# Which queue carries the loads, and where cproj's tiles live, in a fused cross-attention block

## The chip, the core and the metric

The kernel runs on one core of a Trainium2 chip. The metric is the device time of one execution in microseconds, the median of several runs. The engines are TensorE (PE; its weight loads are listed as PEld), VectorE (DVE), ScalarE (ACT), GpSimd (POOL) and SyncE (SP, which only issues DMAs; its queue is listed as SPq).

## The reference

A transformer block with cross-attention, in float32, for 4 batches. Queries and context have 512 rows of 512 features, there are 16 heads of 32, and the inner size of the MLP is 2048:

```python
x = layer_norm(hidden_states, ln1_w, ln1_b)
q = split_heads(x @ q_w + q_b)
k = split_heads(encoder_hidden_states @ k_w + k_b)
v = split_heads(encoder_hidden_states @ v_w + v_b)
attn = softmax(where(mask, q @ k.T / sqrt(32), min))
hidden = merge_heads(attn @ v) @ cproj_w + cproj_b + hidden_states
y = layer_norm(hidden, ln2_w, ln2_b)
return hidden + gelu(y @ fc_w + fc_b) @ proj_w + proj_b
```

## The kernel before, in words

**Groups, tiles, pairs.** The attention work is cut into 16 groups of four heads: group `w` is batch `w // 4`, heads `4 * (w % 4)` on. Each group has four query tiles of 128 rows. For each tile `scores` (L228) multiplies q and k on TensorE (`sc`, L235), VectorE adds the mask and takes the minimum (L240; q is negated, so this is the row's maximum), and ScalarE takes the exponential and its sum (L244). The probabilities must then be transposed for the product with v. In two of the pairs (`ON_PE`) TensorE does that (`turn`, L258) and ScalarE and VectorE copy the result into a `tb` buffer (L261, L263). Everywhere else VectorE transposes blocks of 32 by 32 into `tb` (L272, and L280 for the sums), and then sixteen DMAs per pair of tiles, each of 136 KB, exchange the block rows between partitions (`exchange`, `copies`, L314), from `tb` into `pT`, `gt` or `xe`. A pair is two query tiles, so there are 32 pairs, numbered 0 to 31: pair 7 is the second half of group 3. There are two `tb` buffers, so a new one is free only when the exchange out of an older one has landed. `attend` (L337) multiplies v with the transposed probabilities (`av`, L357), in most cases four tiles after the pair's first tile.

**What runs in between.** Other work is put between the score tiles: the k, q and v products (`prep_k`, `prep_q`, `prep_v`: L196, L205, L217) of later groups, layer norm 1 of the next batch (`ln1`, its transposes `tp` at L137), the cproj products of a finished batch (`cproj`, L390 on), layer norm 2, and the MLP of batches 0 and 1 (`fc` L454, `proj` L464). The order is written out by hand in the lists `first[w]` and `later[w]` (L762 to L833) and run by the loop from L836: each entry has a cost, 3.4 for a chain of matmuls and 0.5 for a set of transposes, and before and after each `turn` the loop runs as many entries as half a tile's share of the group's cost allows. Loads have cost 0. The last two batches' MLPs come after the attention, in a form with fewer products (`last_mlps`).

**Queues.** The exchanges are issued by SyncE. A load is issued by whatever engine `Q[0]` names when the program is written: GpSimd for groups 0 to 3, SyncE from group 4 on (L836 to L839). The first batch's loads are on SyncE. Each engine issues its DMAs in program order, together with its other instructions. On GpSimd these are additions of a bias row (`add_row`, L369, 128 by 512), the bias of v (L224) and the reciprocal root of the layer norms (`ln_rs`). `prep_q` and `prep_v` load the next group's wq and wv right after their own matmuls (L206, L221) since there is one buffer of each; wk has two buffers and is loaded at the head of `A(w)`.

**x, rows and cproj.** Layer norm 1's x tiles are allocated from the pool `tiles`, tag `xn`, four buffers (`load_x`, L152). In group 3 the list ends with `hid_(0, ...)`, which loads the four residual tiles of batch 0 and adds a bias row to each (L371), and then `load_x` of batch 2 (`x1`, L800). cproj of batch 0 works on these residual tiles. For batches 1 and 2 it works on `ct` tiles from a pool with two buffers: two are loaded ahead, and the third and fourth are loaded by GpSimd after the store of the first and second (L400 to L402). Their bias rows are added inside `cproj` (L392 to L394). All four results are stored to a DRAM tensor `xa`, from where `load_yn` (L404) and `load_hid` read them again. cproj's weights `wc` (1 MB) are loaded by GpSimd ahead of group 0 (L835). The MLP's weights pass through a ring of eight 256 KB buffers (`load_mlp`, L439); the first eight, all of fc, are loaded at the end of group 0's list.

Of the kernel before, what the change touches and what calls it, by code (L numbers as in the profile page):

```python
# [36 lines left out]
F32 = mybir.dt.float32  # L37
# [7 lines left out]
P = 128  # L45
B, L, D, H = 4, 512, 512, 16
HD = D // H
INNER = 4 * D
NT = L // P
# [25 lines left out]
def xattn_block(ctx: ExitStack, tc: tile.TileContext, x, encT, mask, q_w, k_w, v_w, c_w, fc_w, p_w, vecs, rows, out):  # L75
    nc = tc.nc
    scale = float(np.float32(1.0) / np.sqrt(HD).astype(np.float32))

    def pools(stack, **bufs):
        return [stack.enter_context(tc.tile_pool(name=n, bufs=k)) for n, k in bufs.items()]  # L80

    const, keep, hids, tiles, small = pools(ctx, const=1, keep=1, hids=6, tiles=4, small=4)
    dram = ctx.enter_context(tc.tile_pool(name="dram", bufs=1, space=bass.MemoryType.DRAM))
# [3 lines left out]
    one, two, kqp, five, six, fws = pools(att, one=1, two=2, kqp=4, five=5, six=6, fws=MW)  # L87
# [9 lines left out]
    wc = one.tile([P, ND, D], F32, tag="wc", name="wc")  # L97
# [7 lines left out]
    S = {}  # L105
    Q = [nc.gpsimd]

    def acc_tile(name):
        return ps_acc.tile([P, D], F32, tag="acc", name=name)
# [61 lines left out]
    def load_mask(b, queue):  # L171
        queue.dma_start(out=m8, in_=mask[b : b + 1, :].broadcast_to([P, L]))

    def make_mb(b):
        mb = one.tile([P, L], F32, tag="mb", name=f"mb_{b}")
        nc.vector.tensor_scalar(mb, m8, 0.0, FMAX, ALU.is_equal, ALU.mult)
        if b + 1 < B:
            load_mask(b + 1, nc.gpsimd)
        S["mb", b] = mb

    def load_w(w, queue=None, names=("wk", "wq", "wv")):

        if w >= NW:
            return
        g = w % NG
        for n, src in (("wk", k_w), ("wq", q_w), ("wv", v_w)):
            if n in names:
                S[n, w] = (two if n == "wk" else one).tile([P, ND, P], F32, tag=n, name=f"{n}_{w}")
                (queue or Q[0]).dma_start(out=S[n, w], in_=src[:, g, :, :])

    def prep_k(w):
        b, g = divmod(w, NG)
        kT = kqp.tile([P, L], F32, tag="kT", name=f"kT_{w}")
        acc = acc_tile(f"acck_{w}")
        for d in range(ND):
            nc.tensor.matmul(acc, S["wk", w][:, d, :], eT[:, d, :], start=(d == 0), stop=(d == ND - 1))  # L196
        nc.scalar.activation(kT, acc, AF.Identity, bias=vec[:, KB + g : KB + g + 1], scale=1.0)
        S["kT", w] = kT

    def prep_q(w):  # L200
        b, g = divmod(w, NG)
        qT = kqp.tile([P, L], F32, tag="qT", name=f"qT_{w}")
        acc = acc_tile(f"accq_{w}")
        for d in range(ND):
            nc.tensor.matmul(acc, S["wq", w][:, d, :], xT[:, d, :], start=(d == 0), stop=(d == ND - 1))  # L205
        load_w(w + 1, names=("wq",))  # L206

        nc.scalar.activation(qT, acc, AF.Identity, bias=qb[:, g : g + 1], scale=-scale)
        S["qT", w] = qT

    def prep_v(w):
        b = w // NG
        v = five.tile([P, NT, P], F32, tag="v", name=f"v_{w}")
        acc = acc_tile(f"accv_{w}")
        for t in range(NT):
            for d in range(ND):
                nc.tensor.matmul(  # L217
                    acc[:, ts(t, P)], eT[:, d, ts(t, P)], S["wv", w][:, d, :],
                    start=(d == 0), stop=(d == ND - 1),
                )  # L220
        load_w(w + 1, names=("wv",))  # L221
        nc.scalar.copy(v, acc.rearrange("p (t f) -> p t f", t=NT))  # L222
        bias = row[:, 2, ts(w % NG, P)]
        nc.gpsimd.tensor_tensor(v, v, bias[:, None, :].broadcast_to([P, NT, P]), ALU.add)  # L224
        S["v", w] = v
# [142 lines left out]
    def add_row(h, i):  # L368
        nc.gpsimd.tensor_tensor(h, h, row[:, i, :], ALU.add)  # L369
# [7 lines left out]
        for t in ts_:  # L377
            add_row(S["hid", b, t], 1 if b else 0)

    def load_ct(b, t, queue=None):  # L380

        if t == 0:
            S["xa", b] = dram.tile([L, D], F32, tag=f"xa{b}", name=f"xa{b}")
        if b == B - 1:
            S["ct", b, t] = tiles.tile([P, D], F32, tag="xn", name=f"ct_{b}_{t}")
        else:
            S["ct", b, t] = two.tile([P, D], F32, tag="ct", name=f"ct_{b}_{t}")
        (queue or Q[0]).dma_start(out=S["ct", b, t], in_=x[b, ts(t, P), :])

    def cproj(b, t):  # L390
        h = S["hid", b, t] if b == 0 else S["ct", b, t]
        if b:  # L392
            for i in range(NT if b == B - 1 else 2) if t == 0 else (t,) if t > 1 and b < B - 1 else ():
                add_row(S["ct", b, i], 0)  # L394
        acc = acc_tile(f"accc_{b}_{t}")
        for g in range(NG):
            nc.tensor.matmul(acc, S["oT", b][:, g, ts(t, P)], wc[:, g, :], start=(g == 0), stop=(g == NG - 1))  # L397
        nc.vector.tensor_tensor(h, acc, h, ALU.add)
        if b:
            (nc.sync if b == B - 1 else nc.gpsimd).dma_start(out=S["xa", b][ts(t, P), :], in_=h)  # L400
            if t + 2 < NT and b < B - 1:
                load_ct(b, t + 2, nc.gpsimd)  # L402

    def load_yn(b):  # L404

        S["yn", b] = [tiles.tile([P, D], F32, tag="xn", name=f"xn2_{b}_{t}") for t in range(NT)]
        for t in range(NT):
            Q[0].dma_start(out=S["yn", b][t], in_=S["xa", b][ts(t, P), :])

    def stat2(b, t):  # L410
# [281 lines left out]
    CHAIN, TURN = 3.4, 0.5  # L692

    def do(fn):
        return [(0.0, fn)]

    def A(w):
        if w >= NW:
            return []
        return do(lambda: load_w(w + 1, names=("wk",))) + [  # L700
            (CHAIN, lambda: prep_k(w)),
            (CHAIN, lambda: prep_q(w)),
            (CHAIN, lambda: prep_v(w)),
        ]

    def C(b):
        return [(CHAIN, lambda t=t: cproj(b, t)) for t in range(NT)]
# [54 lines left out]
    first = [[] for _ in range(NW)]  # L762
    later = [[] for _ in range(NW)]
    x1, x2, x3, x4 = inputs(1)
    load2, k2, q2, v2 = A(2)
    load3, k3, q3, v3 = A(3)
    load4, k4, q4, v4 = A(4)
    first[0] = do(lambda: load_w(2, names=("wk",))) + [(CHAIN, lambda: prep_v(1)), (CHAIN, lambda: prep_q(1))] + x1 + [load2, k2, q2] + do(load_mlp)
    first[1] = x2[:1] + [v2, load3, k3] + x2[1:2] + [q3] + x2[2:] + [v3] + x4 + x3
    first[2] = [load4, q4, k4, v4] + A(5)[:2]  # L770
    first[3] = A(5)[2:] + A(6)
    mlp = []
    for p in range(NORMAL):
# [2 lines left out]
    def some(n):  # L776
        taken, mlp[:n] = mlp[:n], []
        return taken

    def hid_(b, *ts_):  # L780
        return do(lambda: load_hid(b, ts_))

    def ct(b):
        return do(lambda: (load_ct(b, 0), load_ct(b, 1)))

    def yn(b):
        return do(lambda: load_yn(b))
# [9 lines left out]


    x1, x2, x3, x4 = inputs(2)
    first[3] += hid_(0, 0, 1, 2, 3) + x1  # L800
    load, k, q, v = A(7)
    c, t2 = C(0), turns2(0)
    first[4] = [load, k] + x2[:2] + [q] + x2[2:] + [v] + x3[:2] + x4
    later[4] = c[:1] + x3[2:] + c[1:]
    load, k, q, v = A(8)
    first[5] = stat(0, 0, 1) + [load, q] + stat(0, 2, 3) + rs(0) + [k] + norm(0, 0, 1, 2, 3) + [v]
    first[5] += t2 + do(lambda: proj_bias(0)) + some(5)
    load, k, q, v = A(9)
    x1, x2, x3, x4 = inputs(3)
    first[6] = [load, k, q] + some(5) + [v] + x1  # L810
    load, k, q, v = A(10)
    first[7] = [load, k, q] + some(5) + [v]

    load, k, q, v = A(11)
    first[8] = ct(1) + [load, k] + x2[:1] + [q] + x2[1:2] + some(1) + x2[2:] + [v] + x3[:2] + x4
    c = C(1)
    later[8] = c[:1] + x3[2:] + c[1:]
    load, k, q, v = A(12)
    first[9] = [load, q] + some(2) + [k] + some(3) + [v]
    load, k, q, v = A(13)  # L820
    first[10] = [load, k, q] + some(5) + [v] + yn(1)
    load, k, q, v = A(14)
# [2 lines left out]
    first[11] += norm(1, 2, 3) + some(1) + t2 + [v] + some(1)  # L825

    load, k, q, v = A(15)
    c = C(2)
    first[12] = ct(2) + [load, k] + some(3) + hid_(1, 0, 1)
    later[12] = c  # L830
    first[13] = hid_(1, 2, 3) + [q] + some(3) + [v] + some(3)
    first[14] = yn(2) + some(5) + stat(2, 0, 1) + some(2) + stat(2, 2, 3) + rs(2) + some(1)
    first[15] = norm(2, 0, 1) + some(4) + norm(2, 2, 3) + some(4) + turns2(2)  # L833

    nc.gpsimd.dma_start(out=wc, in_=c_w)  # L835
    for w in range(NW):  # L836
        if w and w % NG == 0:
            make_mb(w // NG)
            Q[0] = nc.sync  # L839
        work, rest = first[w], later[w]  # L840
        share = sum(c for c, _ in work + rest) / NT
        due = 0.0
        for qt in range(NT):
            u = w * NT + qt
            pair = AT.get(u, (u - LAG) // 2 if u >= LAG and u % 2 == 0 else None)
            if pair in AT.values() and u not in AT:
                pair = None
            if pair is not None:
                turn_sums(*divmod(pair, 2))
                attend(*divmod(pair, 2))  # L850
            scores(w, qt)

            if qt == 2:
                work, rest = work + rest, []
            due += share / 2
            due -= run(work, due)
            turn(w, qt)
            if u % 2 == 1:
                over_sums(w, qt // 2)
            due += share / 2  # L860
            due -= run(work, due)
        run(work + rest)
    exchange()

    for t in range(NT):
        load_ct(B - 1, t)
    run(some(2))
    turn_sums(NW - 1, 0)
    attend(NW - 1, 0)
# [56 lines left out]
```

## Time and profile before

| | us |
|---|---|
| median of 3 runs (836.4 to 838.74) | 836.82 |
| the profiled execution | 840.83 |
| its span, first to last instruction | 839.0 |
| TensorE busy | 811.6 (97%) |
| VectorE busy | 553.9 (66%) |
| ScalarE busy | 342.5 (41%) |
| GpSimd busy | 119.6 (14%) |
| mean granted TensorE clock | 0.987 |

All places are microseconds from the start of the profiled span. The page cuts the span in 40 slices of 21 us, and gives the busy share of each in tenths. In a timeline each row has the start, the length, the engine, the line, the operation with output and inputs, how many instructions were merged, and in brackets the idle time of the engine just before and what ended it. DMA rows on SPq or POOL are the issuing, not the transfer.

### The profile page before, as it was taken

The page shows a single profiled execution, that of the slowest core. Times are in us where ns is not written, and L with a number is a line of the kernel's source. Part 1 is how long each engine was busy: PE and PEld are TensorE (multiplying, and loading weights), DVE is VectorE, ACT ScalarE, POOL GpSimd, SP SyncE. Part 2 cuts the span into 40 slices and gives each one's busy share as a digit, 9 for nine tenths or more (in the row PEclk, how much of TensorE's full clock was granted, in tenths as well). Part 3 has the DMA queues.
Part 4 walks back from the last instruction along what each step waited for, and adds up shares of the span by engine and source line. Part 5 has one row for each costly group of instructions (what it writes and reads, how often), then busy time and mean ns, then how long its engine had stood idle before and what let it go on. Part 6 is the DMA issues. An engine that isn't in the chain of part 4 may idle for free.

```text
span 839.0 us, 11999 instructions
## 1 busy us (share of the span) xinstructions
PE 811.6 (97%) x4064; PEld 472.3 (56%) x4064; DVE 553.9 (66%) x1259; ACT 342.5 (41%) x740; POOL 119.6 (14%) x152
## 2 busy tenths in 40 slices
PE   9997999499999999999999989999999999999998
PEld 6545544345445454454554435443446888888887
DVE  4595887577666786776787476787425998168511
ACT  2654554134764564356444456464301331023300
POOL 2332214303000013100001321000022003100011
PEclk9997999799999999999999999999999999999999
DMA  5477488565777877587786867985835551032001
GB/s 205 164 194 184 136 243 217 147 165 145 186 189 198 227 198 226 157 211 187 197 240 166 249 167 185 237 194 136 226 119 194 168 181 46 8 94 75 14 14 38
DMA packets 57885, 136.88 MB, mean 163 GB/s; under 512 B 12144, under 2 KB 14320, under 8 KB 57696
## 3 DMA queue, kind: packets, MB, share of 16 engines
q1 hardware_dynamic: 52176, 117.75, 51.9%
q0 software_dynamic: 5120, 17.24, 6.8%
q10 hardware_dynamic: 528, 1.14, 0.6%
q8 instruction: 32, 0.52, 0.3%
q14 instruction: 29, 0.24, 0.1%
HBM read 61.89 MB, written 7.34 MB: 83 GB/s over the span
## 4 chain that ended last, share of the span: by engine, by line
PE 83%; DMA 7%; DVE 5%; SPq 2%; POOL 2%; issue 1%; ACT 0%; DVEq 0%; POOLq 0%
PE accp L464 13%; PE accf L454 12%; PE q L558 12%; PE sc L235 7%; PE av L357 7%; PE accv L217 5%; PE accc L397 5%; PE accq L205 5%; PE acck L196 4%; DMA pT<-tb 2%; PE tp L137 2%; DMA xn<-x_dram 2%; PE q4p L598 2%; PE q6p L598 2%; PE q3p L598 2%; PE q1p L598 2%
## 5 line engine op out<-in xcount | busy, mean ns | idle before, releaser
L244 ACT ACTIVATE s<-s,mn 128x512 f32<-128x512 f32 x256 | 181.6, 711 | 178.4 <-DVE mn L240 178.1
L240 DVE CUSTOM_DVE_ANT_0 s<-sc,mb 128x512 f32<-128x512 f32 x256 | 161.3, 686 | 50.1 <-PE sc L235 50.0
L272 DVE STREAM_TRANSPOSE tb<-s 128x512 f32<-128x512 f32 x240 | 152.6, 684 | 5.6 <-ACT s L244 5.0
L454 PE MATMUL accf<-yT,fcw 128*128 128x512 f32 x256 | 115.3, 600 | 0.4 <-DVE yT L140 0.4
L464 PE MATMUL accp<-pw,gt 128*128 128x512 f32 x256 | 114.3, 598 | 0.0
L454 PEld LDWEIGHTS accf<-yT,fcw 128*128 128x128 f32 x256 | 47.0, 190 | 66.0 <-issue 60.8
L464 PEld LDWEIGHTS accp<-pw,gt 128*128 128x128 f32 x256 | 47.4, 190 | 63.2 <-issue 60.5
L235 PE MATMUL sc<-kT,qT 32*128 32x512 f32 x512 | 73.7, 646 | 2.1 <-DVE mn L240 1.3
L217 PEld LDWEIGHTS accv<-wv,xe 128*128 128x128 f32 x512 | 58.9, 192 | 10.2 <-issue 9.5
L217 PE MATMUL accv<-wv,xe 128*128 128x128 f32 x512 | 60.7, 277 | 0.0
L357 PE MATMUL av<-pT,v 128*32 128x256 f32 x864 | 53.9, 391 | 6.6 <-DMA gt<-tb 3.7
L558 PE MATMUL q<-ys,gt 128*128 128x256 f32 x256 | 60.1, 379 | 0.0
L196 PE MATMUL acck<-xe,wk 128*128 128x512 f32 x128 | 58.7, 601 | 0.0
L205 PE MATMUL accq<-xe,wq 128*128 128x512 f32 x128 | 58.5, 599 | 0.0
L397 PE MATMUL accc<-wc,oT 128*128 128x512 f32 x128 | 57.0, 597 | 0.0
L558 PEld LDWEIGHTS q<-ys,gt 128*128 128x128 f32 x256 | 48.6, 190 | 6.6
L468 DVE TENSOR_TENSOR hid<-accp,hid 128x512 f32<-128x512 f32 x32 | 21.9, 686 | 41.0 <-PE accp L464 39.7
L244 ACT ACTIVATION_READ_ACCUMULATOR s<-s,mn 128x1 f32 x256 | 47.8, 187 | 0.0
L357 PEld LDWEIGHTS av<-pT,v 128*32 128x32 f32 x864 | 26.3, 112 | 36.2 <-issue 17.7
L224 POOL TENSOR_TENSOR v<-v,row 128x512 f32<-128x512 f32 x16 | 20.4, 1274 | 183.3 <-ACT v L222 183.2
L558 PE MATMUL q<-yT,gt 128*128 128x256 f32 x192 | 46.3, 379 | 0.0
L244 ACT ACT_TABLE_LOAD x19 | 24.4, 1283 | 43.7 <-DVE mn L240 43.7
(126 smaller groups left out, 882.2 us busy)
## 6 DMA issues: line engine op xcount, KB each, us to landing
pT<-tb SPq DMA_DIRECT2D x400, 136.0 KB, 2.4
pw<-p_w_dram SPq DMA_DIRECT2D x32, 256.0 KB, 3.8
gt<-fc_w_dram SPq DMA_DIRECT2D x32, 256.0 KB, 2.9
gt<-tb SPq DMA_DIRECT2D x48, 136.0 KB, 3.5
fcw<-fc_w_dram SPq DMA_DIRECT2D x24, 256.0 KB, 3.3
pb<-p_w_dram SPq DMA_DIRECT2D x16, 256.0 KB, 4.1
xe<-tb SPq DMA_DIRECT2D x24, 136.0 KB, 2.4
xe<-encT_dram SPq DMA_DIRECT2D x12, 256.0 KB, 3.9
```

Of the source, the lines that this page charges most:

```text
L196: nc.tensor.matmul(acc, S["wk", w][:, d, :], eT[:, d, :], start=(d == 0), stop=(d == ND - 1))
L205: nc.tensor.matmul(acc, S["wq", w][:, d, :], xT[:, d, :], start=(d == 0), stop=(d == ND - 1))
L217: nc.tensor.matmul(acc[:, ts(t, P)], eT[:, d, ts(t, P)], S["wv", w][:, d, :], start=(d == 0), stop=(d == ND - 1),)
L235: nc.tensor.matmul(sc[:, h, :], qT[r, ts(qt, P)], kT[r, :], start=True, stop=True)
L240: nc.vector.tensor_tensor_reduce(out=s, in0=sc[:, h, :], in1=S["mb", w // NG], scale=1.0, scalar=FMAX, op0=ALU.add, op1=ALU.min, accum_out=mn,
L244: nc.scalar.activation(s, s, AF.Exp, bias=mn, scale=-1.0, accum_out=sums[:, qt, h : h + 1])
L272: nc.vector.transpose(tv[:, q, h], S["ps", w, qt][h])
L357: nc.tensor.matmul(av[ts(h, HD), : 2 * P].rearrange(shape, **kw), v[:, t, ts(h, HD)], p[t][h], start=(t == 0), stop=(t == NT - 1),)
L397: nc.tensor.matmul(acc, S["oT", b][:, g, ts(t, P)], wc[:, g, :], start=(g == 0), stop=(g == NG - 1))
L454: nc.tensor.matmul(acc, S["fcw", b, f][:, d, :], S["yT", b][:, d, :], start=(d == 0), stop=(d == ND - 1))
L464: nc.tensor.matmul(acc, gT[q % 2][:, k, ts(t, P)], S["pw", b, q * FQ + k], start=(k == 0), stop=(k == FQ - 1))
L558: nc.tensor.matmul(o, a[:, k], y[:, k], start=(k == 0), stop=(k == 1))
```

## The change

Six edits; nothing that is computed changes.

1. `Q[0]` becomes SyncE at `w == 1` instead of `w == 4`, so all loads from the second group on are in the queue of the exchanges.
2. `load_x` of batch 2 moves from the end of group 3's list to its head, and the residual rows of batch 0 to the middle of it.
3. The MLP's first eight weights move from the end of group 0's list to its head, in front of the weights of group 2.
4. cproj's weights move from ahead of group 0 to the head of group 2's list.
5. cproj's third and fourth tile of batches 1 and 2 are allocated among layer norm 1's tiles (`xn`) and loaded without waiting for a store, and their bias rows are added at the load. Layer norm 2 uses these two in place, so two of its four reloads are gone.
6. In group 8 the transposes of layer norm 1 are no longer split around the first cproj product, and tiles 2 and 3 are loaded at the end of that list; in group 12 all four are loaded at its head.

```diff
-    def load_ct(b, t, queue=None):
-
-        if t == 0:
-            S["xa", b] = dram.tile([L, D], F32, tag=f"xa{b}", name=f"xa{b}")
-        if b == B - 1:
-            S["ct", b, t] = tiles.tile([P, D], F32, tag="xn", name=f"ct_{b}_{t}")
-        else:
-            S["ct", b, t] = two.tile([P, D], F32, tag="ct", name=f"ct_{b}_{t}")
-        (queue or Q[0]).dma_start(out=S["ct", b, t], in_=x[b, ts(t, P), :])
+    def load_ct(b, *ts_):
+
+        for t in ts_:
+            if t == 0:
+                S["xa", b] = dram.tile([L, D], F32, tag=f"xa{b}", name=f"xa{b}")
+            pool, tag = (tiles, "xn") if b == B - 1 or t > 1 else (two, "ct")
+            S["ct", b, t] = pool.tile([P, D], F32, tag=tag, name=f"ct_{b}_{t}")
+            Q[0].dma_start(out=S["ct", b, t], in_=x[b, ts(t, P), :])
+        for t in ts_:
+            add_row(S["ct", b, t], 0)
 
     def cproj(b, t):
-        h = S["hid", b, t] if b == 0 else S["ct", b, t]
-        if b:
-            for i in range(NT if b == B - 1 else 2) if t == 0 else (t,) if t > 1 and b < B - 1 else ():
-                add_row(S["ct", b, i], 0)
+        h = S["ct" if b else "hid", b, t]
...
         if b:
             (nc.sync if b == B - 1 else nc.gpsimd).dma_start(out=S["xa", b][ts(t, P), :], in_=h)
-            if t + 2 < NT and b < B - 1:
-                load_ct(b, t + 2, nc.gpsimd)
 
     def load_yn(b):
 
-        S["yn", b] = [tiles.tile([P, D], F32, tag="xn", name=f"xn2_{b}_{t}") for t in range(NT)]
-        for t in range(NT):
+        S["yn", b] = [S.get(("ct", b, t)) for t in range(NT)]
+        for t in range(2):
+            S["yn", b][t] = tiles.tile([P, D], F32, tag="xn", name=f"xn2_{b}_{t}")
             Q[0].dma_start(out=S["yn", b][t], in_=S["xa", b][ts(t, P), :])
...
-    first[0] = do(lambda: load_w(2, names=("wk",))) + [(CHAIN, lambda: prep_v(1)), (CHAIN, lambda: prep_q(1))] + x1 + [load2, k2, q2] + do(load_mlp)
+    first[0] = do(load_mlp) + do(lambda: load_w(2, names=("wk",))) + [(CHAIN, lambda: prep_v(1)), (CHAIN, lambda: prep_q(1))] + x1 + [load2, k2, q2]
...
-    first[2] = [load4, q4, k4, v4] + A(5)[:2]
+    first[2] = do(lambda: Q[0].dma_start(out=wc, in_=c_w)) + [load4, q4, k4, v4] + A(5)[:2]
     first[3] = A(5)[2:] + A(6)
...
-    first[3] += hid_(0, 0, 1, 2, 3) + x1
+    first[3] = x1 + first[3][:2] + hid_(0, 0, 1, 2, 3) + first[3][2:]
...
-    first[8] = ct(1) + [load, k] + x2[:1] + [q] + x2[1:2] + some(1) + x2[2:] + [v] + x3[:2] + x4
-    c = C(1)
-    later[8] = c[:1] + x3[2:] + c[1:]
+    first[8] = ct(1, 0, 1) + [load, k] + x2[:1] + [q] + x2[1:2] + some(1) + x2[2:] + [v] + x3 + x4 + ct(1, 2, 3)
+    later[8] = C(1)
...
-    c = C(2)
-    first[12] = ct(2) + [load, k] + some(3) + hid_(1, 0, 1)
-    later[12] = c
+    first[12] = ct(2, 0, 1, 2, 3) + [load, k] + some(3) + hid_(1, 0, 1)
+    later[12] = C(2)
...
-    nc.gpsimd.dma_start(out=wc, in_=c_w)
     for w in range(NW):
         if w and w % NG == 0:
             make_mb(w // NG)
+        if w == 1:
             Q[0] = nc.sync
...
-    for t in range(NT):
-        load_ct(B - 1, t)
+    load_ct(B - 1, *range(NT))
```

More of the change, by code (lines that the diff above doesn't have):

```diff
@@ L781, in hid_, with ct @@
         return do(lambda: load_hid(b, ts_))
-    def ct(b):
-        return do(lambda: (load_ct(b, 0), load_ct(b, 1)))
+    def ct(b, *ts_):
+        return do(lambda: load_ct(b, *ts_))
     def yn(b):
```

## The prediction

> **What bounds the kernel now.** I read the page first (busy shares, slices), then TensorE's waits, then the timelines of TensorE, GpSimd and SyncE where TensorE has holes.
>
> ```profile
> PE 811.6 (97%) x4064; PEld 472.3 (56%) x4064; DVE 553.9 (66%) x1259; ACT 342.5 (41%) x740; POOL 119.6 (14%) x152
> PE   9997999499999999999999989999999999999998
> PEclk9997999799999999999999999999999999999999
> ```
>
> TensorE is busy 811.6 of 839.0 us, and the change keeps its matmuls. So only its holes (27.4 us) and half-clock stretches can be won; they lie in the slices with a 7 and a 4 near the start. TensorE's timeline around the second:
>
> ```profile
> 123.92 3.70 PE L205 MATMUL accq<-xe,wq 128*128 128x512 f32 x8
> ...
> 135.69 1.93 PE L357 MATMUL av<-pT,v 128*32 128x256 f32 x32 [1.37 <-DMA pT<-tb]
> ...
> 146.76 3.84 PE L217 MATMUL accv<-wv,xe 128*128 128x128 f32 x32
> 161.28 2.60 PE L137 MATMUL tp<-ident,xn 128*128 128x128 f32 x8 [10.68 <-DVE xn L128]
> 163.82 2.75 PE L357 MATMUL av<-gt,v 128*32 128x256 f32 x32
> 166.49 1.14 PE L235 MATMUL sc<-kT,qT 32*128 32x512 f32 x8
> ```
>
> It stands 10.68 us for the normalised x of batch 2. GpSimd's timeline says why that came late:
>
> ```profile
> 134.62 0.55 POOL L189 DMA_DIRECT2D wv<-v_w_dram  x1 [6.15 <-PE accv L217]
> ...
> 136.40 2.21 POOL L376 DMA_DIRECT2D hid<-x_dram  x4
> ...
> 146.71 1.27 POOL L369 TENSOR_TENSOR hid<-hid,row 128x512 f32<-128x512 f32 x1 [0.22 <-DMA hid<-x_dram]
> 147.93 2.18 POOL L155 DMA_DIRECT2D xn<-x_dram  x4
> ```
>
> The four loads of x stand behind four row additions, which wait for the hid loads. The earlier hole is in group 1:
>
> ```profile
> 71.68 3.64 PE L357 MATMUL av<-pT,v 128*32 128x256 f32 x32 [2.93 <-DMA gt<-tb]
> 75.25 1.86 PE L235 MATMUL sc<-kT,qT 32*128 32x512 f32 x8
> ```
>
> and SyncE's timeline shows the exchanges of pairs 1, 2, 4, 5, 6, 7, sixteen DMAs each:
>
> ```profile
> 48.89 16.46 SPq L314 DMA_DIRECT2D pT<-tb  x16
> 66.22 11.32 SPq L314 DMA_DIRECT2D gt<-tb  x16
> 98.04 11.06 SPq L314 DMA_DIRECT2D pT<-tb  x16
> 109.60 10.35 SPq L314 DMA_DIRECT2D gt<-tb  x16
> 122.33 10.88 SPq L314 DMA_DIRECT2D pT<-tb  x16
> 137.17 13.41 SPq L314 DMA_DIRECT2D gt<-tb  x16
> ```
>
> Pair 1 takes 16.46 us while GpSimd's eight fc weights (2 MB, issued from 47.19) move; its tb buffer is what the copies out of group 1's transposes wait for. The last hole, 0.68 + 1.54 us near 492 and 502, follows VectorE's two waits in cproj of batch 2:
>
> ```profile
> 473.50 0.69 DVE L398 TENSOR_TENSOR ct<-accc,ct 128x512 f32<-128x512 f32 x1 [4.00 <-POOL ct L369]
> ...
> 485.38 0.69 DVE L398 TENSOR_TENSOR ct<-accc,ct 128x512 f32<-128x512 f32 x1 [5.78 <-POOL ct L369]
> ```
>
> **What the Trainium skill says.** "TensorE: Matmul & The Clock Gate", Part 1: after an idle window of about 3.4 us the clock halves, and about as much sustained work brings it back. The trace agrees roughly: in windows of 2 us the clock falls near 155.3 (idle since 150.6) and is whole again by 166, 5 us after work resumes; in group 1 it is halved from 67 to 76. "DMA: Bandwidth & Descriptors", Issuing engines are not separate DMA queues: all queues share the same 16 engines, and a second issuer saves only issue time. The trace agrees: pair 1 at 16.46 us against 10.35 for pair 5. The same page, Anatomy of one DMA — SWDGE (gpsimd) path: waits for semaphores happen on the issuing sequencer, so a waiting DMA holds all behind it. GpSimd's timeline above is that case.
>
> **The change, part by part.** All places are in the clock of the trace before.
>
> (1) fc's first weights into group 0. They follow wq at 23.9, where cproj's weights (1 MB) stood. Eight issues cost GpSimd 4.30 us, four more than now. Behind them wait wk of group 2 (issued near 28.9 instead of 24.44), then wv, v's bias and x of batch 1, whose own releases (28.8, 35.5) come no earlier. 2 MB at 300 GB/s (the DMA view has 286 to 403 in the slices from 26) lands by 32, wk near 33; its matmuls start at 37.95. Cost 0; without that margin of 5 us each us late is a us. What it frees: pair 1 runs alone, near 10.5 us as pair 5 does, landing by 62, so the copies need not wait. TensorE then gets to av at 68.76 (end of the transposes): 2.93 us. The clock should stay whole: av 3.64 to 1.93 and sc 1.86 to 1.14, 2.4 us. Sum 5.3, between 2.9 (clock still falls, since VectorE's 1.6 us wait before stays) and 5.8.
>
> (2) x ahead of rows. The x loads now follow pair 5 on SyncE at about 120, 27 us sooner. VectorE can do its statistics from 143.7 without a wait, but the tiles are normalised only by 151.6 (3.5 us statistics, 2.5 L240, 1.9 normalising). Alone this would save about 10.9 us there plus up to 2.4 of half clock.
>
> (3) The same loads, and every weight from group 1's v on, in SyncE's queue. This is where I see the gain go. SyncE's order in the changed program: pair 5; x four times, wq and wv for group 6; pair 6; hid four times, wk and wq for group 7; pair 7; wv for group 7. Before, GpSimd issued wq(6) at 112.28 and wv(7) at 134.62, beside the exchanges.
> - wq(6): pair 5 ends near 120.1; four x loads at 0.5 us (two ct loads take 1.08 on SyncE near 459), then wq at 122.2. 1.3 MB plus 0.5 MB of pair 5's tail at 280 GB/s, an estimate between the 250 of contended slices and the 370 of a burst of loads near 462, land at 126.8. Its matmuls were due at 123.92: a new stall of 2.9 us (bounds 0 and 4.5).
> - pair 6 starts at 123 and lands by 136.1; av was due at 134.3 + 2.9 = 137.2, so the old wait of 1.37 is absorbed, and the shift is +1.5.
> - wk(7), behind pair 6 and four hid loads, lands near 140; due 140.1. Nothing taken, bounds 0 and 1.5.
> - pair 7: VectorE's part ends 2.9 later, at 140.0; 10.7 us of issues to 150.7. Only then wv(7), landing 3.3 us later (the median of an exchange DMA there) at 154.0. Due 146.76 + 1.5 = 148.3: a stall of 5.7 us (bounds 3 and 9).
> - Then accv to 157.7, transposes 158.7 (x normalised by 153, so no longer the last to come), av 160.6: sc at 160.6 instead of 166.49. The clock: by the page's 3.4 us, a 5.7 us hole holds a whole window about two times in three (estimate: (5.7 - 3.4) / 3.4), at the 2.4 us of group 1: 1.6. Gain 5.9 - 1.6 = 4.3, bounds 0 and 9.5.
>
> x of batch 3 and all later loads are already on SyncE. wv(3), wk(4), wq(4), wv(4), wk(5), wv(5) are issued behind pairs 1, 2 and 4 but due 3 to 10 us after they land: 0. Moving cproj's weights to group 2: due at 167, 0.
>
> (4) cproj's tiles. ct 2 and 3 are loaded with the first two, not after their stores, so the 4.00 and 5.78 us waits of VectorE go. TensorE's part was 0.68 + 1.54 = 2.2; I take 2.0, bounds 0 and 2.2. In batch 1 (group 8) VectorE waited 4.12 us and TensorE not at all: there ct 2 now comes behind pair 16 and four loads of the encoder, near 332, its row is added by 333.4 and VectorE starts at about the same 334: 0. Two of four reloads of xa per batch go, hidden anyway: 0. Four additions of rows now stand before the stores to xa on GpSimd; their readers come two groups later: 0.
>
> Sum: 5.3 + 4.3 + 2.0 = 11.6 us. The profiled execution took 840.83 us (span 839.0 and 1.8 around it), so it would take 829.2. The median of the runs is 836.82, 4.0 below the profiled one; taking the same 11.6 off gives **825.2 us**.
>
> **Rivals.**
> - *The weights land in time.* If SyncE's loads slip past exchanges cheaply (wq(6) and wv(7) cost under 1.5 us together), the stage gives 12 instead of 4.3: 836.8 - 5.3 - 12 - 2 = 817.5. For it: in later groups weights on SyncE cost TensorE nothing. Against it: there a group lasts 36 us and its weights have slack, here 30 and they are due within 12.
> - *The whole stage is eaten.* wv(7) at its upper bound, pair 7 at 13.41 us as now, and two half-clock stretches: stage 0, group 1 only 2.9: 836.8 - 2.9 - 2 = 832.
> - *SyncE becomes the bound, slower.* Pairs 4 to 7 and 15 loads run in one row from 98.0: wv(7) lands at 98 + 4E + 7 + 3 for E us per exchange, sc follows 9 us later at 117 + 4E, against 166.5 + 7.3 (what (1) and (4) save). It breaks even at E = 14.2 and is over 0.3% slower from 14.8. At 16.46, pair 1's contended time, 4E + 117 = 182.8: 9 us slower, 845.8. For it: 2 MB more than now flow beside pairs 6 and 7. Against: pairs 4 to 6 took 10.4 to 11.1 with loads beside them.
> - *The early weights do nothing.* Pair 1 stays slow for another reason: the 5.3 are lost, 830.5.
>
> **Chances.** Forecast (820 to 829.5) 0.55; weights in time 0.17; stage eaten or early weights useless 0.18; SyncE bound 0.05; the rest 0.05 spread around no change. A difference of 0.3% (2.5 us) is about what a measurement of this kernel can tell from none. Faster 0.90, same 0.04, slower 0.06. The range reaches from the rival with weights in time to the eaten stage: 817 to 832.
>
> **What would show it.** Right: pair 1's sixteen issues in about 10.5 us and no half clock near 70; TensorE's 10.68 us wait for xn gone; in its place accq waiting for wq near 119 and accv waiting for wv near 146 (5 us earlier than above, by (1)); no VectorE wait for ct L369 in batch 2; GpSimd without DMA issues from group 1 to 3. Wrong: TensorE without a wait for a weight between 110 and 155, or exchanges of 14 us and more.

## The result and the profile after

The changed kernel takes 839.56 us (median of 20 runs, 837.88 to 842.1), the kernel before 837.31 (20 runs, 834.91 to 841.03): a ratio of 1.0025 with a 95% interval of 1.0013 to 1.0037. The forecast was 825.2. The profiled execution of the changed kernel took 839.08 us (span 837.3), 1.75 less than the profiled one of before; in the medians it is 2.25 more.

The page of the changed kernel, busy line, slices of TensorE and its clock:

```profile
PE 813.2 (97%) x4064; PEld 473.7 (57%) x4064; DVE 555.6 (66%) x1259; ACT 342.6 (41%) x740; POOL 103.6 (12%) x122
PE   9998979799999989999999999999999999999998
PEclk9999989999999998999999999999999999999999
```

The 4 of before (the 10.68 us hole) has become a 7, but there is a second 7 two slices earlier, and around 315 us an 8 with the clock lowered in the slice after it, where before had 9s. TensorE's timeline of the changed kernel, at these places:

```profile
68.67 1.93 PE L357 MATMUL av<-pT,v 128*32 128x256 f32 x32
...
122.63 6.16 PE L205 MATMUL accq<-xe,wq 128*128 128x512 f32 x8 [4.89 <-DMA wq<-q_w_dram]
...
151.94 5.24 PE L217 MATMUL accv<-wv,xe 128*128 128x128 f32 x32 [5.38 <-DMA wv<-v_w_dram]
...
159.84 1.14 PE L235 MATMUL sc<-kT,qT 32*128 32x512 f32 x8
...
312.01 2.60 PE L137 MATMUL tp<-ident,xn 128*128 128x128 f32 x8 [3.64 <-DVE xn L128]
314.55 3.64 PE L357 MATMUL av<-pT,v 128*32 128x256 f32 x32
318.12 1.44 PE L235 MATMUL sc<-kT,qT 32*128 32x512 f32 x8
```

Read it from the top. Group 1 has no hole and runs at full clock (1.93 for an `av` that took 3.64). Then come the two foretold waits for weights, each followed by a product at half clock (6.16 for 3.70, 5.24 for 3.84). At 159.84 the work is 6.65 us ahead of before (166.49). Then comes a wait that the forecast does not have: in group 8 TensorE stands 3.64 us for the normalised x of batch 3, and the next products run at half clock. Before, the same `tp`, `av` and `sc` had no wait and full clock:

```profile
314.86 1.04 PE L137 MATMUL tp<-ident,xn 128*128 128x128 f32 x8
315.82 1.93 PE L357 MATMUL av<-pT,v 128*32 128x256 f32 x32
317.69 1.14 PE L235 MATMUL sc<-kT,qT 32*128 32x512 f32 x8
```

So 6.65 us ahead became 0.43 behind at that `sc`: 7.1 us are lost in group 8, half of them the wait and half the slower clock. SyncE's timeline of the changed kernel has the reason of the two weights:

```profile
49.28 10.10 SPq L314 DMA_DIRECT2D pT<-tb  x16
...
114.57 2.03 SPq L155 DMA_DIRECT2D xn<-x_dram  x4
116.69 0.38 SPq L189 DMA_DIRECT2D wq<-q_w_dram  x1
...
137.85 10.91 SPq L314 DMA_DIRECT2D gt<-tb  x16
148.87 0.53 SPq L189 DMA_DIRECT2D wv<-v_w_dram  x1
```

Pair 1 takes 10.10 us instead of 16.46, wq of group 6 goes out behind four loads of x, wv of group 7 behind pair 7. And GpSimd's timeline of the changed kernel has the reason of the third:

```profile
305.32 1.26 POOL L369 TENSOR_TENSOR ct<-ct,row 128x512 f32<-128x512 f32 x1 [12.65 <-DMA ct<-x_dram]
307.68 1.26 POOL L369 TENSOR_TENSOR ct<-ct,row 128x512 f32<-128x512 f32 x1 [1.10 <-DMA ct<-x_dram]
309.04 0.19 POOL L122 TENSOR_SCALAR ve<-mv 128x4 f32<-128x4 f32 x1
309.31 1.03 POOL L124 TENSOR_TENSOR rs<-ve,nhalf 128x4 f32<-128x4 f32 x1
```

Edit 5 adds the bias rows to all `ct` tiles where they are loaded. For the first two tiles of batch 1 that is the head of group 8's list. Their additions stand on GpSimd ahead of the reciprocal root of layer norm 1 (`ve`, `rs`), and wait for loads that SyncE issues only at 302.61, behind the exchange of pair 15. VectorE idles 6.61 us for `rs`, TensorE for VectorE. Before, the same two additions came after `rs`:

```profile
308.24 1.03 POOL L124 TENSOR_TENSOR rs<-ve,nhalf 128x4 f32<-128x4 f32 x1
...
317.01 2.50 POOL L369 TENSOR_TENSOR ct<-ct,row 128x512 f32<-128x512 f32 x2
```

At the end, batch 2's cproj has no VectorE wait for the row additions, and both of TensorE's holes there (0.68 and 1.54 us) are gone: the changed kernel is 0.74 behind at the `sc` of 484.63 (483.89 before), level at 492.77, and 1.6 ahead where the last part starts (638.69 instead of 640.30).

### The profile page after: what moved, and what is told of

Read it like the earlier page. It is cut to its first block, busy times and chain, and to the rows that moved or that the text cites. A ratio compares the mean times of both kernels' runs of the same rounds, so it can differ in the third digit from the quotient of the medians.

```text
span 837.3 us, 11995 instructions
## 1 busy us (share of the span) xinstructions
PE 813.2 (97%) x4064; PEld 473.7 (57%) x4064; DVE 555.6 (66%) x1259; ACT 342.6 (41%) x740; POOL 103.6 (12%) x122
## 4 chain that ended last, share of the span: by engine, by line
PE 89%; DVE 4%; SPq 3%; DMA 3%; issue 1%; POOL 0%; ACT 0%; DVEq 0%; ACTq 0%; POOLq 0%
PE accp L461 13%; PE accf L451 13%; PE q L555 12%; PE sc L235 7%; PE av L357 7%; PE accc L395 7%; PE accq L205 6%; PE accv L217 5%; PE acck L196 5%; SPq L314 3%; PE tp L137 2%; PE q4p L595 2%; PE q3p L595 2%; PE q5p L595 2%; PE q6p L595 2%; PE q1p L595 2%
## 5 line engine op out<-in xcount | busy, mean ns | idle before, releaser
L217 PEld LDWEIGHTS accv<-wv,xe 128*128 128x128 f32 x512 | 60.2, 196 | 15.2 <-issue 13.9
L205 PE MATMUL accq<-xe,wq 128*128 128x512 f32 x128 | 60.9, 621 | 4.9 <-DMA wq<-q_w_dram 4.9
L205 PEld LDWEIGHTS accq<-xe,wq 128*128 128x128 f32 x128 | 24.5, 198 | 39.1 <-issue 34.9
```

The source lines that it names most:

```text
L217: nc.tensor.matmul(acc[:, ts(t, P)], eT[:, d, ts(t, P)], S["wv", w][:, d, :], start=(d == 0), stop=(d == ND - 1),)
```

## The experiments

**Group 8.** First the changed kernel with one entry of a list moved:

```diff
-    first[8] = ct(1, 0, 1) + [load, k] + x2[:1] + [q] + x2[1:2] + some(1) + x2[2:] + [v] + x3 + x4 + ct(1, 2, 3)
+    first[8] = [load, k] + x2[:1] + [q] + x2[1:2] + some(1) + x2[2:] + ct(1, 0, 1) + [v] + x3 + x4 + ct(1, 2, 3)
```

> The changed kernel, with the first two ct tiles of batch 1 (loads and row additions) moved in group 8 from ahead of layer norm 1's work to behind its last transposes. Theory (group 8: the row additions wait on GpSimd for the ct loads, with layer norm 1's reciprocal root behind them, and TensorE stands 3.64 us for the normalised x and then runs at half clock): the wait for xn near 312 is gone, the half clock after it too, sc and av there at full clock, and the time falls by about 7 us against the changed kernel, to 832.5, 0.6% below the kernel before. Rival (the 7.1 us that group 8 takes go to something else, such as more work in that list or bandwidth): the hole moves or stays, and the time is within 2 us of the changed kernel's 839.6.

834.25 us (7 runs; ratio to the kernel before 0.997, interval 0.9954 to 0.9985), 5.3 below the changed kernel. GpSimd's timeline of this kernel:

```profile
304.02 1.03 POOL L124 TENSOR_TENSOR rs<-ve,nhalf 128x4 f32<-128x4 f32 x1
311.08 2.52 POOL L369 TENSOR_TENSOR ct<-ct,row 128x512 f32<-128x512 f32 x2 [6.03 <-DMA ct<-x_dram]
```

The root now comes before the additions, and TensorE's `tp` takes 1.04 us without a wait. The theory holds; the size is 5.3 instead of 7. The two profiled executions differ by 4.3 us: this one is 2.4 behind at the `sc` near 160 (162.26 instead of 159.84), where the program is the same and only the execution differs (the wait for wq was 6.27 us instead of 4.89, and the product after wv took 6.56 instead of 5.24). So group 8 itself gave 6.8 in this pair. Why the medians show 5.3 is not shown.

The converse is the kernel before with edits 5 and 6 alone (the lines of `load_ct`, `cproj`, `load_yn`, `first[8]`, `first[12]` and their `later` in the diff).

> The kernel before with edits 5 and 6 alone (cproj's third and fourth tile among layer norm 1's tiles, row additions at the load, group 8's order). Theory: group 8 loses what the changed kernel lost there, a wait for the normalised x of 3.6 us and a half clock, 5 to 7 us, and group 12 gains 1.6 to 2: 3 to 5 us slower than the kernel before. Rival (group 8's loss in the changed kernel came with its 6.65 us lead, not with the row additions): within 2 us of the kernel before.

842.67 us (11 runs; 1.007, 1.0048 to 1.0091): 6.0 slower than the kernel before, 1 more than the most that was expected. The wait for xn in group 8 is 2.75 us, the half clock follows it, and the additions stand ahead of `rs` with 12.88 us of idle time. In this trace a wait of 1.68 us comes on top, at 355.59, for the exchange of group 8's second pair, which neither the kernel before nor the changed one has. The rival falls by the medians: up to group 8 the two programs are the same, so neither of them leads there on average. The traces alone would not have settled it, since the profiled execution of this kernel was by chance 4.8 us ahead of that of before at the `sc` of 166.49.

**Group 1.** The kernel before with edits 3 and 4 alone:

```diff
-    first[0] = do(lambda: load_w(2, names=("wk",))) + ... + [load2, k2, q2] + do(load_mlp)
+    first[0] = do(load_mlp) + do(lambda: load_w(2, names=("wk",))) + ... + [load2, k2, q2]
-    first[2] = [load4, q4, k4, v4] + A(5)[:2]
+    first[2] = do(lambda: Q[0].dma_start(out=wc, in_=c_w)) + [load4, q4, k4, v4] + A(5)[:2]
-    nc.gpsimd.dma_start(out=wc, in_=c_w)
```

> The kernel before with edits 3 and 4 alone: fc's first weights at the head of group 0's list, cproj's weights in group 2. Theory: pair 1's exchange is alone, its issues take about 10.5 us instead of 16.5, the 2.93 us hole of group 1 and the half clock after it go, and the time falls by 5.3 us (bounds 2.9 and 5.8) against the kernel before. Rival (the profiled execution of the kernel before was an unlucky one, 3.5 us above its median, and the hole in group 1 with its half clock is not in most executions): the time falls by less than 2 us.

834.16 us (22 runs; 0.9956, 0.9944 to 0.9969), 3.05 less: near the theory's lower bound, and more than the rival's 2. In the trace the hole and the half clock are gone (`sc` at 70.22 instead of 75.25, 5.0 us). To see how usual that hole is, the kernel before was profiled again, unchanged:

> The kernel before, unchanged, profiled once more, since its first profiled execution was 3.5 us above its median. If that execution was unlucky in a place that the forecast counted on: the hole and half clock of group 1 (2.93 and 2.4 us) or the 10.68 us wait for xn are smaller by some 3.5 us in all. If the 3.5 us are spread over many waits: both stay within 1 us.

841.76 us, with a hole of 3.82 us in group 1, a half clock after it, and 10.57 for xn. Both stayed within 1 us, but this execution was as slow as the first, so it does not tell where a usual one is shorter. Two other kernels do the same work up to 80 us. The one with edits 5 and 6 alone has this there:

```profile
69.50 1.93 PE L357 MATMUL av<-pT,v 128*32 128x256 f32 x32 [1.30 <-DMA gt<-tb]
```

1.30 us, and no half clock. The one with edit 2 alone (below) has 1.86 us and a half clock. From the `sc` near 58.5 to the `sc` after the hole, these four executions took 5.2, 5.5, 1.4 and 4.1 us longer than the one with edits 3 and 4 (in the order above). So what edit 3 saves differs from one execution to the next.

The half clock is not all due to the exchange, either. In the profiled execution of before, from TensorE's timeline and from the view by windows of 2 us, where the third number from the end is the clock:

```profile
64.95 2.41 PE L258 MATMUL tpp<-ident,s 128*128 128x128 f32 x12 [1.60 <-ACT s L244]
```

```profile
66.00:68.00 2.00, 1.67 (x9) 1.03 (x8) 0.00 (x0) 1.58 (x5) 0.00 (x0) 0.63 1.01 257
```

The clock fell between 66 and 67 us, behind a wait of 1.60 us for ScalarE; the hole that pair 1's exchange makes began only at 68.75. With edit 2 alone it was the same. That wait of 1.60 us is in all fourteen traces, and the clock fell behind it in these two, in none of the ten traces with edit 3. Two of four against none of ten does not show that edit 3 keeps the clock whole there.

The spread is in the runs, too: over 44 runs of the kernel before, those with a mean granted clock of 0.994 took 835.4 us on average (7 runs), those with 0.988 took 839.2 (4 runs). The profiled execution of before, at 0.987 and 3.5 us above the median, was near the slow end.

**Group 3.** The kernel before with edit 2 alone, x ahead of rows and both on GpSimd:

```diff
-    first[3] += hid_(0, 0, 1, 2, 3) + x1
+    first[3] = x1 + first[3][:2] + hid_(0, 0, 1, 2, 3) + first[3][2:]
```

> The kernel before with edit 2 alone: the four loads of x of batch 2 stand ahead of batch 0's residual rows, on GpSimd as before. Theory: TensorE's 10.68 us wait for xn goes, with the half clock after it, no weight is late, and the time falls by 10 to 13 us against the kernel before. Rival (another wait takes its place at once, for instance VectorE's own work or wv of group 7 behind the hid loads and rows on GpSimd): the time falls by less than 6 us.

838.42 us (22 runs; 1.0022, 1.001 to 1.0034): no gain at all, 1.2 more. The theory fell; the rival (less than 6 us) stands, but with neither of the waits that it named. TensorE's timeline of this kernel:

```profile
117.04 3.64 PE L357 MATMUL av<-pT,v 128*32 128x256 f32 x32 [5.80 <-DMA gt<-tb]
...
147.47 3.64 PE L357 MATMUL av<-pT,v 128*32 128x256 f32 x32 [6.98 <-DMA gt<-tb]
```

The 10.68 us wait for xn is gone, and two waits for exchanges, 12.78 us together, each with a half clock, stand in its place. x (1 MB) is now in flight beside pair 4, and the residual rows (1 MB) beside pair 6. The DMA views from 96 to 160 us, number of issues, size and median time to landing, of the kernel before and then of this one:

```profile
pT<-tb SPq DMA_DIRECT2D x32, 136.0 KB, 3.5
```

```profile
pT<-tb SPq DMA_DIRECT2D x32, 136.0 KB, 5.9
```

From 112 to 120 us the DMA engines of this kernel are busy all the time (shares of 1.04 and 1.03, 256 and 259 GB/s), and TensorE stands from 111.2 to 117.04. The changed kernel with edit 1 undone says the same:

```diff
-        if w == 1:
+        if w == NG:
```

> The changed kernel with edit 1 undone: the loads of groups 1 to 3 are issued by GpSimd again, x ahead of rows and all else as changed. Theory (wq and wv of groups 6 and 7 wait on SyncE behind the exchanges): TensorE's waits for wq (4.9 us) and wv (5.4 us) and their half clocks (2.5 and 1.4 us) go; group 8's wait stays; the time falls by 7 to 11 us against the changed kernel, to 829 to 832.5. Rival (the waits for the weights come from bandwidth, not from SyncE's order): the waits stay within 2 us of their size and the time within 2 us of 839.6.

841.58 us (6 runs; 1.0063, 1.0038 to 1.0087), 2.0 more than the changed kernel, where 7 to 11 less were expected. Both waits for weights went, as the theory had it, but waits of 5.63 and 6.42 us for exchanges came instead. Neither theory had that. The new one: between 96 and 160 us exchanges and loads share one set of DMA engines, busy for 79 to 82% of that stretch in the four traces (before, changed, edit 2 alone, edit 1 undone), and the queue mainly decides which of them is late. This is what the Trainium skill says in "DMA: Bandwidth & Descriptors", Issuing engines are not separate DMA queues, with a sharper edge: there a second issuer gains little; here it makes two waits of 5.6 to 7 us, since it puts loads in flight beside a more urgent exchange. SyncE's row, where loads and exchanges follow each other, kept `pT` at a median of 2.8 us to landing and made the weights late.

Three kernels between these ends start from the changed one. Only wq of group 6 and wv of group 7 on GpSimd:

```diff
-                (queue or Q[0]).dma_start(out=S[n, w], in_=src[:, g, :, :])
+                q = nc.gpsimd if (n, w) in (("wq", 6), ("wv", 7)) else queue or Q[0]
+                q.dma_start(out=S[n, w], in_=src[:, g, :, :])
```

> The changed kernel with two loads of 256 KB, wq of group 6 and wv of group 7, issued by GpSimd as before; x of batch 2, the residual rows and all others stay on SyncE. Order theory (SyncE's queue makes them late): TensorE's waits for wq and wv and their half clocks go, the exchanges beside them are hardly slower since only 0.5 MB moves beside 4 MB, and the time falls by 6 to 10 us against the changed kernel's 839.6. Bandwidth theory (loads and exchanges share a rate, so whatever is moved out of the queue delays an exchange): waits for gt or pT of 2 to 4 us each appear in their place, and the time falls by less than 5 us.

831.91 us (7 runs; 0.9948, 0.9928 to 0.9967), 7.7 below the changed kernel by medians: the order theory's size. The waits for wq and wv are gone; one wait of 4.18 us for pair 6's exchange came, with a half clock, as the bandwidth theory had it. Half a megabyte on the other queue costs less than all loads of groups 1 to 3 there (841.58 us). Then x alone moved to where the changed kernel's DMA engines are idle (from 84 to 92 us their busy share is 0.22 and then 0.00):

```diff
+    x1, x2, x3, x4 = inputs(2)
-    first[2] = do(lambda: Q[0].dma_start(out=wc, in_=c_w)) + [load4, q4, k4, v4] + A(5)[:2]
+    first[2] = do(lambda: Q[0].dma_start(out=wc, in_=c_w)) + [load4, q4] + x1 + [k4, v4] + A(5)[:2]
...
-    x1, x2, x3, x4 = inputs(2)
-    first[3] = x1 + first[3][:2] + hid_(0, 0, 1, 2, 3) + first[3][2:]
+    first[3] = first[3][:2] + hid_(0, 0, 1, 2, 3) + first[3][2:]
```

> The changed kernel with the four loads of x of batch 2 (1 MB) moved from the head of group 3's list into group 2's, behind group 4's q, where the trace of the changed kernel has the DMA engines idle for 9 us. Bandwidth theory (groups 3's traffic is the limit: x delays an exchange on GpSimd, a weight on SyncE): the wait for wq of group 6 falls from 4.9 us to under 1, its half clock of 2.5 goes, the wait for wv stays near 5, and the time falls by 5 to 8 us against 839.6. Order theory alone (the weight waits for the exchange, not for x): the wait for wq falls by at most the 2.0 us that x's issues take, and the time by at most 2 us.

830.85 us (6 runs; 0.9934, 0.9918 to 0.995), 8.7 below. The wait for wq falls to 0.87 us, though wq still goes out right behind pair 5: its delay came from the x loads ahead of it, not from the exchange. Two things were not foretold. A wait of 2.98 us for wk of group 7, behind the residual rows, came new; and the wait before the product with wv, expected to stay near 5 us, fell to 2.40, still with a half clock after it. The three mends together (the list of group 8, x in group 2, and of the two loads on GpSimd only wv of group 7):

> The changed kernel with three edits: the ct tiles of batch 1 behind layer norm 1 in group 8, x of batch 2 in group 2, and wv of group 7 on GpSimd. If each wait has the cause given to it: -5 for group 8, -5 to -8 for wq and -5 to -7 for wv, 820 to 825 in all. If wv on GpSimd is late as well (behind the four residual row additions that wait for their loads) or delays pair 7: 826 to 830.

825.84 us (5 runs; 0.9865, 0.9845 to 0.9884), between the two expectations. wv on GpSimd was not late. Pair 7's issues took 13.15 us, as the second expectation had it, but its `av` did not wait. What was late is wk of group 7, behind the residual rows, which neither had. TensorE's timeline:

```profile
135.92 5.37 PE L197 MATMUL acck<-xe,wk 128*128 128x512 f32 x8 [4.10 <-DMA wk<-k_w_dram]
```

So the residual rows were moved to the idle stretch too:

```diff
-    first[2] = ... + [load4, q4] + x1 + [k4, v4] + A(5)[:2]
+    first[2] = ... + [load4, q4] + x1 + do(lambda: load_hid(0, range(NT))) + [k4, v4] + A(5)[:2]
-    first[3] = first[3][:2] + hid_(0, 0, 1, 2, 3) + first[3][2:]
```

> The kernel with three mends (ct tiles behind layer norm 1 in group 8, x of batch 2 in group 2, wv of group 7 on GpSimd), with the four residual tiles of batch 0 (1 MB) loaded in group 2 as well, right behind x. There TensorE waited 4.10 us for wk of group 7, which stood on SyncE behind these four loads, and ran at half clock after it. Bandwidth theory: that wait goes with its half clock, pair 7's sixteen issues take 11 us instead of 13.15, and the time falls by 4 to 7 us from 825.8, to 819 to 822. Rival (the megabyte now delays pair 4 or a weight of group 4 or 5 by as much): within 2 us of 825.8.

820.51 us (6 runs; 0.9804, 0.9775 to 0.9834), 5.3 less. The page of this kernel:

```profile
PE 806.1 (99%) x4064; PEld 470.9 (58%) x4064; DVE 555.6 (68%) x1259; ACT 342.3 (42%) x740; POOL 104.1 (13%) x123
PE   9998999999999999999999999999999999999998
PEclk9999999999999999999999999999999999999999
```

One 8 is left besides the last slice, and no slice with a lowered clock: the mean clock is 1.000. Last, the same two loads in group 2, but with all loads of groups 1 to 3 on GpSimd, group 8 first as changed and then mended:

> The changed kernel with edit 1 undone (loads of groups 1 to 3 on GpSimd) and x of batch 2 and the residual tiles of batch 0 both loaded in group 2; group 8 is as changed, with its wait. With edit 1 undone alone the time was 841.6, with waits for gt of 5.6 and 6.4 us. Bandwidth theory (x delayed pair 4 and the residual tiles pair 6 because they were in flight together; the queue they are issued from only decides who is delayed): both waits and their half clocks go, 12 to 15 us, to 827 to 830. Queue theory (loads issued by GpSimd delay exchanges wherever they stand, or SyncE's order is what matters): at most half of that goes, and the time stays above 834.

827.9 us (6 runs; 0.9894, 0.9867 to 0.9922): 13.7 less than with edit 1 undone alone, and no wait for an exchange over 1.6 us. For x and the residual rows the bandwidth theory holds.

> The kernel with the loads of groups 1 to 3 on GpSimd and x and the residual tiles in group 2 (827.9), and in group 8 the ct tiles behind layer norm 1. If the mend of group 8 is worth the same here as in the changed kernel (5.3): 822 to 823.5, so that edit 1, the loads in the exchange's queue, is worth at most some 2 us against 820.5, once x and the residual tiles have left the crowded stretch. If edit 1 matters by itself: 825 or more.

821.94 us (5 runs; 0.9812, 0.9788 to 0.9836), so the mend of group 8 is worth 6.0 here, a second time. Its interval overlaps that of the 820.51 (where wv of group 7 is on GpSimd and all other loads of groups 1 to 3 on SyncE): with the two megabytes out of the crowded stretch, the worth of edit 1, the queue, cannot be told from nothing. No run has wv of group 7 on SyncE there.

## Why the prediction was wrong

The terms, in us, negative for a gain; by the traces from the lead of one over the other at the same instruction:

| term | forecast | pair of traces | runs |
|---|---|---|---|
| (1) group 1 | -5.3 | -4.7 | -3.05 (edits 3 and 4 alone) |
| (2), (3) groups 3 to 4 | -4.3 | -1.9 | -0.7, what is left |
| (4) group 8 | 0 | +7.1 | +6.0 with group 12 (edits 5 and 6 alone) |
| (4) group 12 | -2.0 | -2.4 | |
| sum | -11.6 | -1.75 | +2.25 |

In the traces' column 0.3 more is lost between 318 and 484 us; the rest is after 640 us and rounding. The -0.7 assumes that the edits' shares add up. Two other runs agree with it: edit 2 alone cost 1.2, and undoing edit 1 in the changed kernel cost 2.0, so both edits together give about -0.8.

- *The step that failed is in (4).* It costed group 8 by "VectorE starts at about the same 334: 0" and "Four additions of rows now stand before the stores to xa on GpSimd; their readers come two groups later: 0". It looked at the last two tiles and at the stores, and never placed the additions for the first two, which edit 5 moves to the head of group 8, on GpSimd's program: ahead of `rs`, with their own wait for a load. Moving them behind layer norm 1 in the changed kernel, and putting edits 5 and 6 alone into the kernel before, show it from both sides (5.3 and 6.0 us). The forecast had described this very mechanism in group 3, where the x loads stand on GpSimd behind four row additions that wait for loads, and did not ask where its own change puts such additions. Every sign of being right that the forecast named was there; it had named none for group 8. No rival had it; the one rival that was slower, SyncE as the bound, did not happen (the exchanges of pairs 4 to 7 took 10.05 to 12.73 us to issue).
- *(3), mechanism right, a term too small.* wq of group 6: 2.9 forecast, 4.89 measured, and a half clock of 2.46 (6.16 - 3.70) that the sum did not have. It landed 5.9 us after its issue instead of the reckoned 4.6; pair 6's exchange went out at 117.64, right behind it, and shared the engines, which is the likely reason but was not tried alone. wv of group 7: 5.7 forecast, 5.38 measured; half clock 1.6 and 1.4. The forecast charged the order on SyncE and the bytes ahead. For wq the runs charge the bytes (4.89 to 0.87 us without x ahead of it). For wv they agree with the order: it went out right behind pair 7's last issue, and with wv of group 7 on GpSimd its wait was gone. What the forecast did not see, in (2) too, is that the same bytes on GpSimd make the exchanges late instead.
- *(2) alone* would not have saved its 10.9: 838.42 us. That number was reckoned as if x's landing beside pair 4 were free. (By the forecast's own places, 161.28 and 151.6, the wait would have shrunk by 9.7; the sum does not use either.)
- *(1), mechanism right for the hole, not shown for the clock.* Pair 1 took 10.10 us for the forecast 10.5, and the hole went. But 5.3 was the loss of one execution; over many runs it is 3.05. And the forecast took the half clock from 67 to 76 as agreeing with an idle window of about 3.4 us. In that trace it does not: the clock fell before the 2.93 us hole, when TensorE's last wait had been the one of 1.60 for which the forecast set its lower bound of 2.9.
- *The base.* Taking a saving that was read from an execution at 840.83 off a median of 836.82 assumed that the usual execution has the same holes. 4.0 us of the 13.9 between forecast gain and measured loss are this: the traces differ by -1.75, the medians by +2.25. It is no further cause beside the table but the difference of its last two columns, 1.65 of it in group 1.
- *(4), group 12* came as forecast: 2.4 us (0.74 up to 492.77 and 1.6 after it) for 2.0.

What stays open: which holes the usual execution of the kernel before lacks besides that of group 1 (only profiled executions have a trace); why moving group 8's additions gives 5.3 us by medians where the trace has 7.1; and whether wv of group 7 would still be late on SyncE with both megabytes gone.

## What to carry to other kernels

When a step moves on an in-order engine, place every instruction that it issues, with the load it waits for, against what follows it there: two cheap additions of 1.26 us held a 1 us root, and through it TensorE, and took back most of what the rest of the change had gained in the profiled pair (7.1 of 9.0 us). Where transfers crowd a stretch, changing the queue of all loads chose what was late (839.56 and 841.58 us). Moving two loads alone helped, and left a wait of 4.18 us. Moving bytes to an idle stretch (here 2 MB, from beyond 114 us to 84) took the waits away, on either queue. And a saving read from one profiled execution counts against that execution, not against the median: look at the clock of the runs first.

## What the runs showed of the hardware

The length of a hole alone does not say whether the clock falls. The wait of 1.60 us in group 1, at the same instruction of the same work, was followed by a fall of the clock within about 2 us in two of fourteen traces, and by none in twelve. A wait of 2.75 us (group 8, edits 5 and 6 alone) was followed by half clock for about 4 us, and one of 2.98 (x in group 2, wk of group 7) left the clock whole. The Trainium skill, "TensorE: Matmul & The Clock Gate", Part 1, speaks of windows of about 3.4 us of activity that the hardware watches; the clock fell here after holes shorter than that, so a bound of 3.4 us on one hole is not safe. And the DMA engines moved 227 to 278 GB/s where their busy share was 1.0 in windows of 4 us between 96 and 156 us, with exchanges of 136 KB and loads of 256 KB. A load put into such a stretch showed as another transfer's delay: with edit 2 alone, `pT` took a median of 5.9 us to land instead of 3.5.
